# A two-layer graph transformer on one core: v and half of q in another PSUM pool, weights on a second queue, a drained first block and a light second one

## The chip, the core and the metric

The kernel runs on one core of one Trainium2 chip. A core has TensorE (matrix products into PSUM), VectorE, ScalarE and GpSimd for the rest, and SyncE, which here only issues transfers. Each engine carries out its own instructions in order. Transfers are issued from the instruction streams of SyncE, ScalarE and GpSimd; an issue that has to wait holds up what stands behind it in that stream. The metric is device time in microseconds (us), the median of three runs.

## What is computed

Two graph-transformer layers on 2708 tokens of width 512, 8 heads of 64, an adjacency matrix (int32, 2708 x 2708) as mask, and a feed-forward part of width 2048:

```python
mask = adj.astype(jnp.float32) + jnp.eye(n, dtype=jnp.float32)
q = (h @ Wq.T + bq).reshape(n, N_HEADS, D_K)
k = (h @ Wk.T + bk).reshape(n, N_HEADS, D_K)
v = (h @ Wv.T + bv).reshape(n, N_HEADS, D_K)
scores = jnp.einsum('nhd,mhd->hnm', q, k) / jnp.sqrt(jnp.float32(D_K))
scores = jnp.where(mask[None, :, :] == 0, jnp.float32(-1000000000.0), scores)
attn = jax.nn.softmax(scores, axis=-1)
ctx = jnp.einsum('hnm,mhd->nhd', attn, v).reshape(n, D_MODEL)
h1 = _layer_norm(h + ctx @ Wo.T + bo, ln1_g, ln1_b)
ff = jax.nn.relu(h1 @ W1.T + b1) @ W2.T + b2
h2 = _layer_norm(h1 + ff, ln2_g, ln2_b)
```

(The line of `h1` joins two lines of the reference.) An entry of the matrix is set with probability of about 0.3%, so a token has few neighbours.

## The kernel before, in words

The work is done per tile of 128 tokens: 22 tiles, the last with 20. Attention is not a matrix product here. For each token the kernel lists its neighbours, sorts the tokens by the length of their lists, and gathers the k and v rows of the neighbours. A place in the list is a slot; tile g of the sorted order has `CAPS[g]` slots, 22 for tile 0 down to 3 for tile 21. An attention step ("chunk") takes up to two slots: GpSimd gathers kv rows (`gather`, L948), VectorE multiplies with q and sums per head (L987, L993), ScalarE takes exponentials (L1006) and scales v (L1013), VectorE scales one slot and adds (L1019, L1026). Behind a tile's last chunk come `sums` (L1034 to L1049) and `divided` (ScalarE, L1057), which leaves `cx`. `loads` gathers up to three chunks ahead, into five buffers.

The program has these stages.

- **Keys** (`first`, layer 0). For each tile, k and v by `project` (L565), each four matmuls of 128x512 into one PSUM tile with tag "g", of which there are three (`ps`). VectorE adds the bias to k (L834), ScalarE copies v (L836) and issues the store of the row pair. Beside this the adjacency rows come in (L652), GpSimd adds the diagonal (L653), ScalarE squares them into codes (L657), and VectorE finds the largest codes (`lists`, L660 to L667). When all tiles have their lists, `counted` and `ranked` compute each token's rank; 22 indirect transfers (L765) scatter the lists to their places in DRAM, one load reads them back (L776), and `ident_i` (L791) then says which token stands where.
- **Queries** (`first_queries`, layer 0). q for all tiles in their original order, biased by VectorE (L880) and stored in pairs (`written`, L868). At tile 9 (`OWN`) the rows of the first block's tokens (`xr`, gathered by `ident_i`) are transposed and their queries computed, at tile 11 those of the second block, which go to the table `q_own`. `beside_queries` loads w1 and w2, advances the attention and, at tiles 17 and 18, starts the first block's attended part.
- **Blocks**, for each layer: the sorted tiles in pairs, 11 blocks. Block 0 is (21, 20), 148 tokens; the others have 256. The attended part of a block (`attended`): `cx` transposed, multiplied by Wo (o), residual and norm. The feed-forward part (`feed_forward`): 16 steps f, each four matmuls into a PSUM tile pf of tag "f" (three of them, pool `ps_f`), ReLU by ScalarE into ft (L1266), and with a lag of three steps two matmuls of W2 into the sums a0 and a1 (L1246). Within the steps of block k the attention of the block after it is moved on: `advance` gives it credit, at most two finished tiles may stand ready, and at f = 10 `through(k + 1)` takes what is missing. In layer 0, `keys_values` makes k and v of the layer after it from the finished block.
- **Between the layers**: the queries of the first 8 sorted tiles from preloaded `zT` tiles, then 8 more by `queries`, each with a load of `zT` from DRAM, a projection, VectorE's bias (L1191) and a store.

TensorE, ScalarE and SyncE run in the order in which the program is written. VectorE and GpSimd are ordered by a scheduler, except where the program names them too (GpSimd in the first two stages, VectorE in the queries stage and between the layers). The order of the blocks and the drain of the attention stand in these lines:

```python
blocks = [(NT - 1, NT - 2)] + [
    (i, NT - 3 - i) for i in (*range(5, 8), *range(5), *range(8, NT // 2 - 1))
]
```

So block 1 is (5, 14), with 11 + 8 = 19 slots, and (0, 19), with 28, is block 4. A projection's four matmuls show as eight records in the trace.

## Time and profile before

| | us |
|---|---|
| median of 3 runs | 2006.14 (2004.35 to 2006.95) |
| the profiled execution | 2007.56 |
| its span, first to last instruction | 2005.7 |
| TensorE busy | 1910.0 |
| VectorE busy | 1302.4 |
| ScalarE busy | 935.2 |
| GpSimd busy | 800.3 |

The mean granted clock of TensorE is 0.983 of its full rate. The transfers moved 367.98 MB, 183 GB/s on average, but 322 and 348 GB/s in the first two stretches of 50 us, where the adjacency rows come in. Of the chain of work that ended last the trace gives only the end, some 4 us: the second tile's norm, its `rd` on GpSimd, and the store of the output. Busy times of several engines lie beside each other and don't add up to the span; where TensorE is idle, the trace names what released it (`<-`), and that is how its rows are read: start, length, engine, line, operation, how many records, and in brackets the idle time before them with its releaser.

### The profile page before, as it was taken

The page shows a single profiled execution, that of the slowest core. Times are in us where ns is not written, and L with a number is a line of the kernel's source. Part 1 is how long each engine was busy: PE and PEld are TensorE (multiplying, and loading weights), DVE is VectorE, ACT ScalarE, POOL GpSimd, SP SyncE. Part 2 cuts the span into 40 slices and gives each one's busy share as a digit, 9 for nine tenths or more (in the row PEclk, how much of TensorE's full clock was granted, in tenths as well). Part 3 has the DMA queues.
Part 4 walks back from the last instruction along what each step waited for, and adds up shares of the span by engine and source line. Part 5 has one row for each costly group of instructions (what it writes and reads, how often), then busy time and mean ns, then how long its engine had stood idle before and what let it go on. Part 6 is the DMA issues. An engine that isn't in the chain of part 4 may idle for free. (4 is left out here: it accounts for less than half of the span.)

```text
span 2005.7 us, 20899 instructions
## 1 busy us (share of the span) xinstructions
PE 1910.0 (95%) x6162; PEld 1102.3 (55%) x6162; DVE 1302.4 (65%) x2140; ACT 935.2 (47%) x3219; POOL 800.3 (40%) x708
## 2 busy tenths in 40 slices
PE   8989887999999999999999996999999999999996
PEld 3434334556655566556566642456666666666664
DVE  6874387866878668477542027697699879776421
ACT  4560145563664537446432112566467555664310
POOL 3104345544645436345210023454385546544110
PEclk9999998999999999999999998999999999999998
DMA  8985768545566456455310647666467556454000
GB/s 321 349 296 193 253 227 320 184 160 194 173 210 200 164 177 198 138 181 167 128 56 19 220 153 256 216 211 219 152 220 242 195 172 231 163 184 147 27 11 13
DMA packets 131615, 367.98 MB, mean 183 GB/s; under 512 B 16796, under 2 KB 36620, under 8 KB 128782
## 3 DMA queue, kind: packets, MB, share of 16 engines
q0 software_dynamic: 69104, 246.35, 36.7%
q1 hardware_dynamic: 59332, 109.10, 15.8%
q10 hardware_dynamic: 3054, 11.09, 1.4%
q8 instruction: 50, 0.82, 0.2%
q14 instruction: 75, 0.61, 0.1%
HBM read 315.14 MB, written 51.35 MB: 183 GB/s over the span
## 5 line engine op out<-in xcount | busy, mean ns | idle before, releaser
L948 POOL DMA_INDIRECT kv<-kv_d,idx x420 | 552.0, 1314 | 501.9 <-DVE acc L1026 343.8
L1246 PE MATMUL a<-w,ft 128*128 128x512 f32 (+1 forms) x1408 | 666.3, 598 | 2.0 <-ACT ft L1266 1.3
L1258 PE MATMUL pf<-hT,w 128*128 128x256 f32 (+1 forms) x2816 | 636.9, 373 | 22.0 <-ACT ft L1266 14.8
L1258 PEld LDWEIGHTS pf<-hT,w 128*128 128x128 f32 x2816 | 520.7, 191 | 202.4 <-issue 106.3
L1246 PEld LDWEIGHTS a<-w,ft 128*128 128x128 f32 (+1 forms) x1408 | 255.6, 186 | 227.2 <-issue 203.1
L1266 ACT ACTIVATE ft<-pf,b 128x256 f32<-128x256 f32 (+1 forms) x352 | 157.6, 459 | 426.5 <-PE pf L1258 419.5
L987 DVE TENSOR_TENSOR kv<-kv,q 128x1024 f32<-128x1024 f32 (+3 forms) x222 | 256.6, 1159 | 147.2 <-DMA kv<-kv_d,idx 130.9
L1013 ACT ACTIVATE kv<-kv,p 128x64 f32<-128x64 f32 x1232 | 311.1, 335 | 5.0
L993 DVE TENSOR_REDUCE sc<-kv 128x16 f32<-128x1024 f32 (+3 forms) x222 | 254.8, 1153 | 1.2
L1026 DVE TENSOR_TENSOR acc<-acc,kv 128x1024 f32<-128x1024 f32 (+2 forms) x178 | 204.0, 1146 | 38.7 <-ACT kv L1013 37.5
L1006 ACT ACTIVATE p<-sc,minus 128x8 f32<-128x8 f32 (+1 forms) x420 | 103.5, 295 | 204.4 <-DVE sc L993 178.7
L1086 POOL TENSOR_TENSOR rd<-va,mhalf 128x1 f32<-128x1 f32 (+1 forms) x88 | 81.5, 927 | 283.5 <-DVE va L1084 281.3
L1019 DVE TENSOR_TENSOR kv<-kv,p 128x512 f32<-128x512 f32 (+1 forms) x178 | 121.7, 684 | 74.2 <-ACT p L1006 74.2
L565 PE MATMUL o<-wo,cT 128*128 128x512 f32 (+1 forms) x352 | 155.1, 593 | 0.5 <-ACT cT L1101 0.5
L565 PEld LDWEIGHTS o<-wo,cT 128*128 128x128 f32 (+1 forms) x352 | 65.1, 186 | 86.5 <-issue 74.2
L1057 ACT ACTIVATE cx<-acc,su 128x64 f32<-128x64 f32 (+1 forms) x352 | 88.6, 334 | 33.7 <-DVE su L1049 30.1
L1277 DVE TENSOR_TENSOR h<-a,h 128x512 f32<-128x512 f32 (+1 forms) x44 | 28.9, 680 | 111.7 <-PE a L1246 111.7
L1090 DVE SCALAR_TENSOR_TENSOR h<-h,rd,ln_b 128x512 f32<-128x512 f32 (+1 forms) x88 | 65.8, 748 | 53.2 <-POOL rd L1086 53.2
L660 DVE MAX8 tops<-code 128x8 f32<-128x247 f32 (+2 forms) x242 | 82.9, 402 | 19.0 <-ACT code L657 18.8
L657 ACT ACTIVATE code<-aj 128x2708 bf16<-128x2708 int32 (+1 forms) x22 | 73.2, 3328 | 45.5 <-POOL aj L653 41.3
L1316 POOL DMA_INDIRECT kv_d<-kvs,ident_i x22 | 22.9, 1042 | 179.1 <-ACT kvs L1310 117.8
L1013 ACT ACTIVATE acc<-kv,p 128x64 f32<-128x64 f32 (+1 forms) x352 | 88.8, 335 | 1.4
(132 smaller groups left out, 1531.0 us busy)
## 6 DMA issues: line engine op xcount, KB each, us to landing
aj<-in_adj SPq DMA_DIRECT2D x21, 1354.0 KB
w<-in_W SPq DMA_DIRECT2D x32, 512.0 KB
kv_d<-kvs ACTq DMA_DIRECT2D x21, 512.0 KB
xg<-in_xT SPq DMA_DIRECT2D x20, 512.0 KB
kv<-kv_d,idx POOLq DMA_INDIRECT x420
q_d<-qs SPq DMA_DIRECT2D x22, 256.0 KB
zT_d<-zT SPq DMA_DIRECT2D x22, 256.0 KB
xb_d<-h SPq DMA_DIRECT2D x21, 256.0 KB
```

Source lines behind the costliest of these rows:

```text
L565: nc.tensor.matmul(o[:r], xs(c), wm[:, c, :], start=(c == 0), stop=(c == NC - 1))
L948: nc.gpsimd.indirect_dma_start(out=to, out_offset=None, in_=table[:, :], in_offset=bass.IndirectOffsetOnAxis(ap=s, axis=0), bounds_check=N ...
L987: nc.vector.tensor_tensor(kv[:r, :c, :DM], kv[:r, :c, :DM], self.q[:r].unsqueeze(1).to_broadcast([r, c, DM]), ALU.mult,)
L993: nc.vector.tensor_reduce(self.sc[:r, s0 : s0 + c, :], kv[:r, :c, :DM].rearrange("p s (h d) -> p s h d", d=DK), AX.X, ALU.add,)
L1006: nc.scalar.activation(p[:r, s, :], self.sc[:r, s, :], AF.Exp, bias=minus[:r, g, s : s + 1])
L1013: nc.scalar.activation(to[:, i, hd], kv[:r, i, DM + h * DK : DM + (h + 1) * DK], AF.Copy, scale=p[:r, s0 + i, h : h + 1],)
L1019: nc.vector.tensor_tensor(to[:, 0, :].rearrange("p (h d) -> p h d", d=DK), kv[:r, 0, DM:].rearrange("p (h d) -> p h d", d=DK), p[:r, s0, : ...
L1026: nc.vector.tensor_tensor(self.acc[:r, :c, :], self.acc[:r, :c, :], kv[:r, :c, DM:], ALU.add)
L1057: nc.scalar.activation(cx[:r, hd], self.acc[:r, 0, hd], AF.Copy, scale=self.su[:r, h : h + 1])
L1246: nc.tensor.matmul(a[:r], fts[f][:, c0 : c0 + r], self.w2[f // 2][:, f % 2, :], start=(f == 0), stop=(f == NFC - 1),)
L1258: nc.tensor.matmul(pf[:, :w], self.w1[f // 2][:, c, f % 2 * P : f % 2 * P + P], hT[:, c, :w], start=(c == 0), stop=(c == NC - 1),)
L1266: nc.scalar.activation(ft[:, :w], pf[:, :w], AF.Relu, bias=self.b1[:, f : f + 1])
```

## The change

- **PSUM.** v of every tile in the keys stage, and q of every second tile in the queries stage, go to pool `ps_f` (tag "f") instead of `ps`; pf takes 512 columns there, as they do.
- **Order in the first stages.** The transposition of `bk` comes behind the first k; `ranked` comes behind the last tile's k instead of the tile before it; `written` stores a pair of q at the next even tile instead of two pairs later, ahead of that tile's load of tokens.
- **Queues.** w1 and w2 are loaded from the last two tiles of the keys on (parts 0 and 1, SyncE) and in the first three of the queries (parts 2 to 4, ScalarE), instead of at every second query; Wk and Wv of the layer after it go on ScalarE, each in one transfer.
- **Blocks.** Block 1 is (19, 18), with 13 slots. Behind block 0's last tile three empty steps let its attention finish before the next tile begins. The first block's attended part starts at tiles 15 and 16 of the queries instead of 17 and 18.
- **Between the layers**, `zT` is loaded three ahead instead of two.
- **End of a block.** The last three steps of W2 are done per tile: all of a0, then all of a1.

```diff
...
     def chunked(ap):
         return ap.rearrange("(c p) n -> p c n", p=P)
 
-    def matrix(w, name, tag):
+    def matrix(w, name, tag, by=None):
         src = chunked(w[name])
         t = wts.tile([P, src.shape[1], src.shape[2]], F32, tag=tag, name=tag)
+        if by:
+            by.dma_start(out=t, in_=src)
+            return t
         k = max(1, src.shape[1] // 4)
         for c in range(0, src.shape[1], k):
             nc.sync.dma_start(out=t[:, c : c + k, :], in_=src[:, c : c + k, :])
...
             nc.tensor.matmul(pr[:, c * P : (c + 1) * P], ones, dg[:, c, :], start=True, stop=True)
         nc.vector.tensor_copy(t, pr)
 
-    def project(xs, r, wm, name):
-
-        o = ps.tile([P, DM], F32, tag="g", name=name)
+    def project(xs, r, wm, name, other=False):
+
+        o = (ps_f if other else ps).tile([P, DM], F32, tag="f" if other else "g", name=name)
         for c in range(NC):
             nc.tensor.matmul(o[:r], xs(c), wm[:, c, :], start=(c == 0), stop=(c == NC - 1))
         return o
...
         wk = matrix(w, "Wk", "wk")
         turning = turned_row(cols[1], "bk", 1.0)
         bk = next(turning)
-        finish(turning)
         wv = matrix(w, "Wv", "wv")
         pa = tc.tile_pool(name="pa", bufs=2)
         lists, counted, ranked, listed = lists_of(pa.__enter__())
...
             xs = tokens(t, 0)
             kv = wts.tile([P, 2 * DM], F32, tag=f"w2_{5 + t % 3}", name="kvs")
             k = project(xs, r, wk, "k")
+            if t == 0:
+                finish(turning)
             nc.vector.tensor_tensor(kv[:r, :DM], k[:r], bk[:r], ALU.add)
-            v = project(xs, r, wv, "v")
+            if t == NT - 1:
+                ranked(*counts)
+            v = project(xs, r, wv, "v", other=True)
             nc.scalar.copy(kv[:r, DM:], v[:r])
             if before:
                 nc.scalar.dma_start(**before)
...
                 if done == NT:
                     counts = counted()
             meanwhile(t)
-            if t == NT - 2:
-                ranked(*counts)
             if t == QT:
                 wq = matrix(w, "Wq", "wq")
                 turning = turned_row(cols[0], "bq", DK**-0.5)
...
 
         for t in range(NT):
             r = size(t)
-            q = project(tokens(t, 1), r, wq, "q")
+            if t % 2 == 0 and made:
+                written()
+            q = project(tokens(t, 1), r, wq, "q", other=t % 2 > 0)
             if t % 2 == 0:
                 qs = wts.tile([P, 2, DM], F32, tag=f"w2_{5 + t // 2 % 3}", name="qs")
                 made.append((t, qs))
             nc.vector.scalar_tensor_tensor(
                 qs[:r, t % 2], q[:r], DK**-0.5, bq[:r], ALU.mult, ALU.add
             )
-            if len(made) > 2:
-                written()
             if t == OWN - 1:
                 listed()
                 pa.__exit__(None, None, None)
...
-        def load_w1(self, j):
+        def load_w1(self, j, by=nc.sync):
             t = wts.tile([P, NC, 2 * P], F32, tag=f"w1_{j}", name="w1")
-            nc.sync.dma_start(
+            by.dma_start(
                 out=t, in_=chunked(self.w["W1"])[:, :, 2 * P * j : 2 * P * (j + 1)]
             )
             self.w1.append(t)
 
-        def load_w2(self, j):
+        def load_w2(self, j, by=nc.sync):
             t = wts.tile([P, 2, DM], F32, tag=f"w2_{j}", name="w2")
-            nc.sync.dma_start(out=t, in_=chunked(self.w["W2"])[:, 2 * j : 2 * j + 2, :])
+            by.dma_start(out=t, in_=chunked(self.w["W2"])[:, 2 * j : 2 * j + 2, :])
             self.w2.append(t)
 
         def load_second(self, part, temp):
...
 
             zTs = []
             for i in range(len(tiles) + 1):
-                while len(zTs) < min(i + 2, len(tiles)):
+                while len(zTs) < min(i + 3, len(tiles)):
                     zT = dn.tile([P, NC, P], F32, tag="cT", name="zT", bufs=3)
                     nc.sync.dma_start(out=zT, in_=zT_d[self.n][tiles[len(zTs)]])
                     zTs.append(zT)
...
             accs = [ps_a.tile([P, DM], F32, tag=f"a{i}", name=f"a{i}") for i in range(len(block))]
             fts = []
 
-            def second(f):
+            def second(f, only=None):
                 c0 = 0
                 for g, a in zip(block, accs):
                     r = size(g)
+                    if only not in (None, g):
+                        c0 += r
+                        continue
                     nc.tensor.matmul(
                         a[:r],
                         fts[f][:, c0 : c0 + r],
...
                     c0 += r
 
             for f in range(NFC):
-                pf = ps_f.tile([P, 2 * P], F32, tag="f", name="pf")
+                pf = ps_f.tile([P, DM], F32, tag="f", name="pf")
                 for c in range(NC):
                     nc.tensor.matmul(
                         pf[:, :w],
...
                 if f >= LAG:
                     second(f - LAG)
                 yield None
-            for f in range(NFC - LAG, NFC):
-                second(f)
+            for g in block:
+                for f in range(NFC - LAG, NFC):
+                    second(f, g)
             zs = []
             for g, a, h in zip(block, accs, hs):
                 r = size(g)
...
     now = Layer(0, layers[0])
 
 
-    blocks = [(NT - 1, NT - 2)] + [
-        (i, NT - 3 - i) for i in (*range(5, 8), *range(5), *range(8, NT // 2 - 1))
+    blocks = [(NT - 1, NT - 2), (NT - 3, NT - 4)] + [
+        (i, NT - 5 - i) for i in (*range(8, 5, -1), *range(6))
     ]
     NB = len(blocks)
     order = [g for block in blocks for g in block]
...
         peak = small.tile([P, NT], F32, tag="peak", name="peak", bufs=1)
         nc.vector.memset(peak, 0.0)
         loaded = loads(n)
-        steps = [(g, s0, c, i) for g in order for i, (_, s0, c) in enumerate(chunks_of(g))]
+        steps = []
+        for g in order:
+            cuts = chunks_of(g)
+            steps += [(g, s0, c, i, i + 1 == len(cuts)) for i, (_, s0, c) in enumerate(cuts)]
+            if g == order[1]:
+                steps += [None] * 3
+        steps += [None] * 3
         kv = next(loaded)
         yield 0.0
         q = asked(n, order[0])
-        done = []
-        for k in range(len(steps) + 3):
-            if k < len(steps):
-                g, s0, c, i = steps[k]
+        done = [None] * 3
+        for k, step in enumerate(steps):
+            if step:
+                g, s0, c, i, last = step
                 if i == 0:
                     t = Tile(g, q)
                 if k > 0:
...
                 t.weights(kv, s0, c)
                 if i == 1 and g != order[-1]:
                     q = asked(n, order[order.index(g) + 1])
-                done.append((t, kv, s0, c, i + 1 == len(chunks_of(g))))
-            if 0 < k <= len(steps):
-                t1, kv, s0, c, _ = done[k - 1]
-                t1.weigh(kv, s0, c)
-            if 1 < k <= len(steps) + 1 and done[k - 2][-1]:
-                done[k - 2][0].sums(peak)
-            if k > 2 and done[k - 3][-1]:
-                t3 = done[k - 3][0]
-                got[t3.g] = t3.divided()
-            yield steps[k][2] / SLOTS if k < len(steps) else 0.5
+                done.append((t, kv, s0, c, last))
+            else:
+                done.append(None)
+            t3, t2, t1 = done[-4:-1]
+            if t1:
+                t1[0].weigh(*t1[1:4])
+            if t2 and t2[-1]:
+                t2[0].sums(peak)
+            if t3 and t3[-1]:
+                got[t3[0].g] = t3[0].divided()
+            yield c / SLOTS if step else 0.2
...
             now.load_first()
         if t > NT - 3:
             now.load_second(t + 2 - NT, temp)
+            now.load_w1(t + 2 - NT)
+            now.load_w2(t + 2 - NT)
 
     def beside_queries(t):
 
-        if t % 2 == 0 and len(now.w2) < 5:
-            now.load_w1(len(now.w1))
-            now.load_w2(len(now.w2))
+        if len(now.w2) < 5:
+            now.load_w1(len(now.w1), nc.scalar)
+            now.load_w2(len(now.w2), nc.scalar)
         if t > OWN:
-            advance(1.0 if t < NT - 5 else 0.6)
-        if t == NT - 5:
+            advance(1.0 if t < NT - 7 else 0.45)
+        if t == NT - 7:
             through(0)
             early[0] = now.attended(blocks[0], got)
             next(early[0])
-        if t == NT - 4:
+        if t == NT - 6:
             for _ in blocks[0]:
                 next(early[0])
 
...
                 if not last:
                     if (k, f) == (0, 10):
                         now.load_next()
-                        now.kv = [matrix(nxt.w, "Wk", "wk")]
-                    if (k, f) == (0, 14):
-                        now.kv.append(matrix(nxt.w, "Wv", "wv"))
+                        now.kv = [matrix(nxt.w, "Wk", "wk", nc.scalar)]
+                    if (k, f) == (0, 13):
+                        now.kv.append(matrix(nxt.w, "Wv", "wv", nc.scalar))
                     if (k, f) == (3, 2):
                         now.wq = matrix(nxt.w, "Wq", "wq")
                     if f == 1 and k in (1, 3):
```

## The prediction

> **What bounds the kernel now.** I read the page first, then the windows by stage, then TensorE's waits and the timelines of its longest ones.
>
> ```profile
> PE 1910.0 (95%) x6162; PEld 1102.3 (55%) x6162; DVE 1302.4 (65%) x2140; ACT 935.2 (47%) x3219; POOL 800.3 (40%) x708
> ...
> PEclk9999998999999999999999998999999999999998
> ```
>
> TensorE is busy for 1910.0 of 2005.7 us, and the change removes no matmul. So at most the 95.7 us of TensorE idle time can go, and what low clock adds behind it. The windows say where it lies (edges: first query matmul, first matmul of layer 0's feed-forward part, its second block, layer 1's first queries, its feed-forward part, that part's middle, the last matmul). After the window's edges and length come TensorE's busy us, its matmuls, then the other engines; PEclk is the first figure after POOL.
>
> ```profile
> 0.00:178.59 178.59, 162.57 (x376) 70.18 (x376) 134.71 (x470) 84.36 (x44) 29.34 (x68) 0.99 0.83 297
> 178.59:304.35 125.76, 107.72 (x257) 44.30 (x256) 64.66 (x92) 30.05 (x118) 58.85 (x57) 0.95 0.71 237
> 304.35:376.40 72.05, 62.48 (x224) 30.81 (x225) 57.62 (x80) 38.63 (x152) 43.63 (x35) 0.91 0.81 287
> 376.40:1188.83 812.43, 804.61 (x2681) 486.20 (x2680) 481.44 (x694) 375.82 (x1375) 311.13 (x250) 1.00 0.47 158
> 1188.83:1269.97 81.14, 62.79 (x145) 26.13 (x143) 50.32 (x71) 20.47 (x83) 27.09 (x24) 0.89 0.59 204
> 1269.97:1310.00 40.03, 37.55 (x154) 20.44 (x154) 32.87 (x41) 31.37 (x127) 21.41 (x18) 1.00 0.90 296
> 1310.00:1989.90 679.90, 672.30 (x2329) 424.19 (x2328) 475.97 (x684) 354.50 (x1323) 305.01 (x254) 1.00 0.47 158
> ```
>
> Length minus busy: 16.0, 18.0, 9.6, 7.8, 18.4, 2.5, 7.6 us, and 15.8 behind the last matmul. Three quarters of the span hold only 15.4 us; the change must earn its gain in the seams. TensorE's timeline there (idle before, and releaser, in brackets; one projection is 8 records, 3.43 us apart when nothing waits):
>
> ```profile
> 205.95 10.57 PE L565 MATMUL q<-wq,xg 128*128 128x512 f32 x24 [3.05 <-DVE qs L880]
> 221.94 0.58 PE L1096 MATMUL tp<-ident,xr 20*128 20x20 f32 x4 [5.43 <-DMA xr<-in_x,ident_i]
> 296.58 5.24 PE L565 MATMUL q<-wq,xg 128*20 128x512 f32 x8 [4.36 <-DVE h L1219]
> 331.49 2.34 PE L1258 MATMUL pf<-hT,w 128*128 128x148 f32 x8 [6.57 <-ACT ft L1266]
> 1228.52 5.26 PE L565 MATMUL q<-wq,zT 128*128 128x512 f32 x8 [11.70 <-DMA zT<-zT_d]
> ```
>
> The second line hides a chain that is independent of TensorE's pace; GpSimd's timeline shows it:
>
> ```profile
> 173.98 1.11 POOL L765 DMA_INDIRECT rec_d<-rec,ranks  x1 [18.40 <-DVE ranks L761]
> 205.02 1.50 POOL L776 DMA_DIRECT2D new<-rec_d  x1 [3.12 <-DMA rec_d<-rec,ranks]
> 215.01 0.48 POOL L791 CAST ident_i<-new 128x22 int32<-128x22 f32 x1 [7.92 <-DMA new<-rec_d]
> ```
>
> Ranks, 22 scatters 1.28 us apart, a read-back, the cast, the gather of `xr`: 48 us from 173.98 to the flip at 221.94.
>
> **The change, step by step**
>
> **A. Up to the first flip.** Keys: v moves to the other three PSUM buffers, so k and v no longer wait for each other's evacuation. Nine such waits (2.94 at 63.1, then 0.2 to 1.4 each) go: 9.2 us, plus 1.8 for the half-speed matmuls at 63.11 (5.40 us for 8 records against 3.60). Moving `bk`'s transposition behind the first k gives under 1 us, since the 4.7 us before it cover the weights' arrival. But this does not reach the end. The ranks need VectorE's `before` (done at 165.5), and the lists before it are paced by the adjacency rows (DMA 83% busy in that window), which the change doesn't touch. What shifts: the rank matmuls ran at 169.75 behind a v; now they stand behind the short k of the last tile, which is done by then, and start when k's evacuations free PSUM, at about 166.5. VectorE then has two bias sums and one evacuation (0.7 us each, now ahead of the ranks) before the ranks: about 170.5 instead of 173.5, **-3 us**. A read-back now meets less traffic: the loads of w1/w2 stood at 206 and 211 to 214, and now all go out by about 180. The 7.92 us wait is bounded by itself above and by the 3.12 us of the scatters' landing below; I take 5, so **-3 us**. Flip at about 216. TensorE has its ten queries done near 205 (start 171, 10 x 3.43; the 3.05 us wait goes because `written` stores a pair two tiles earlier, so buffers return; SyncE now waits at that store for VectorE's qs with the next xg load behind it, which is for queries four tiles, 13.7 us, later), and waits some 11 us instead of 5.4. So 14 us of gains upstream become 6. A: **-6** (-3 to -10).
>
> Two rules of the Trainium skill weigh here. The page "DMA: Bandwidth & Descriptors", section "Issuing engines are not separate DMA queues", says that DMAs from ScalarE and SyncE share the same DMA engines, so a second issuer saves issue time only. By it, w1/w2 on ScalarE's queue are worth their issue (0.5 us each on SyncE, hidden): nothing. The rows agree on bandwidth, but the timing moves: 3 MB leave the window of the read-back, and that is the 3 us above; by the rule alone A is -3. The other, "TensorE: Matmul & The Clock Gate", section "What's actually happening", has the clock halve after an idle window of about 3.4 us. By it, the short waits cost no clock. The rows differ: after 2.94 us at 63.1, and after only 1.75 us at 271.75, 8 records took 5.40 and 5.16 us. I follow the rows: each removed wait of 2 us or more brings 1.6 to 1.8 us more.
>
> **B. First flip to the first feed-forward matmul (82.4 us).** The first block's drain takes two steps of the third tile (kv x q and its sum, 2 x 2.44 us at 257 and 261) from in front of its last sums, so `cx` is ready near 262 on the old clock (268.5 before) and the attended part can start two tiles earlier, behind q of tile 15 (262.4). Then q16, two o, and q17 to q21 (17.2 us) cover the norm chain (15 us from the last o to h: 285.2 to 300.3), which two queries could not. Gone: 0.34 + 1.75 + 1.6 (clock) + 4.36 + 1.6 (clock) + 1.07 + 0.4 = **-11** (-5 to -13). New coupling: q of odd tiles holds `ps_f` buffers that the first three pf need; VectorE's order puts q21's evacuation some 3 us behind its matmul: below 1 us.
>
> **C. Layer 0's first block.** 9.6 us of waits for ft plus about 4.6 of low clock (320.0 to 337.5). ScalarE stood behind p, p behind VectorE, VectorE 7.21 us behind the gather of q, which waits for every q_d store. The next block is now (19, 18): 13 slots instead of 19, its queries from `q_own`. But the gather for tile 8 follows in the same stretch, at about the same distance from the last store (VectorE evacuates q21 some 3 us into the block). I keep 6 of 14: **-8** (-2 to -13).
>
> **D. Layer boundary.** TensorE needs 36.2 us from 1216.7 to 1252.9 for four projections (13.7): 17.3 of waits, 4.6 of clock. Looking three ahead, zT of the third query loads with the first two (1193.6), and the 11.70 goes. The load after it now needs TensorE to free the first's buffer, and SyncE holds the q_d stores behind it meanwhile; both come from work that precedes it. What is late next: the evacuations. `query` still has only three PSUM buffers, and in the changed order VectorE does three chunks of tile 19 before it frees the preloaded queries' buffers (19.5 us of its work from 1208 put these at about 1217 and 1228 to 1230). I get waits of 4, 8.7 and 1.5 us, the last projection ending near 1244.3, less 1.6 for clock: **-7** (0 to -17).
>
> **E.** Layer 1's first block: one 2.48 us wait for ft, fewer slots: -1 (+2 to -2.5).
>
> **F.** Tail: summing per tile lets the first tile finish 1.7 us earlier (4 records of 0.43), so its store leaves GpSimd free before the second's `rd` (it stood from 1993.9 to 1995.3): -1.5 (-0.5 to -2.5). **Elsewhere** the blocks' order changes; the heavy tile 0 now has 29 slots in its block instead of 28; wk and wv go on ScalarE, 0.5 us of issue each with one ft behind; summing per tile wants the last ft 1.7 us sooner, still 3.4 us behind its pf: 0 (-6 to +6).
>
> **Sum:** -6 - 11 - 8 - 7 - 1 - 1.5 = -34.5. The profiled execution took 2007.56 us (span 2005.7 and 1.9 around it): 1973. It lay 1.4 above the median shown, 2006.14, so I predict **1971 us**.
>
> **Rivals**
> 1. *The waits go whole* (24%). For: each has a named cause that an edit meets. Against: VectorE's order at the boundary. A -8, B -11, C -13, D -14, E -2, F -2: -50, 1956 us.
> 2. *They are only replaced* (12%). q's gather still holds C, PSUM holds D, the read-back is no faster: A -3, B -11, C -2, D 0, F -1.5: -17.5, 1988 us.
> 3. *VectorE becomes the bound in the middle* (4%): slower. A chunk costs it 4.4 us (1.16 + 1.15 + 0.68 + 1.15 by its rows, and idle); 29 slots are 15 chunks, 65 us, and norms and evacuations some 16: 81 of a block's 82. Place: blocks 2 to 10 in both layers, where the backlog starts one light block later. With 3.5 us per block in place of the 15.4 us there now: 18 x 3.5 - 15.4 - 34.5 = +13, 2019 us. It decides above 2.8 us per block (49.9 / 18). Against: only the heavy block showed such waits (2.2 and 2.3 us).
> 4. *The drain doesn't drain* (2%): in the changed VectorE order tile 19's chunks still stand before the last sums at the boundary. Then D is 0 or worse and B half: -20, 1986 us.
>
> **How the numbers follow.** Likeliest 58%, rivals as above. Its own range is 1962 to 1982. With rivals 1, 2 and 4, and the bounds of A, C and D (all good -58, all poor -8), the 8-in-10 range is 1950 to 1990. What a measurement can tell from no change is 0.2%, 4 us. Faster 0.94, same 0.02, slower 0.04.
>
> **What would show it.** A: first flip near 216 with a wait of about 11 us, rank scatters from 171; a flip at 222 refutes it, one below 210 means the lists were not DMA-paced. B: 71 us from flip to feed-forward, no wait at q21. C: a wait for ft below 6 us. D: no wait on zT's DMA above 2 us, instead VectorE's qs as releaser. F: 14 us behind the last matmul. It is wrong if windows of the middle blocks show more than 15 us of new idle time.

## The result, and the profile after

| | before | after |
|---|---|---|
| time, median of 4 runs each | 2006.55 us (2004.35 to 2008.01) | 1983.8 us (1979.94 to 1985.18) |
| after / before | | 0.9884, 95% interval 0.9867 to 0.9902 |
| span of the profiled execution | 2005.7 us | 1982.0 us |

The time lies inside the range and in the forecast direction; 34.5 us were forecast for the profiled span and 23.7 came. The first line of the page of after:

```profile
PE 1903.5 (96%) x6162; PEld 1104.5 (56%) x6162; DVE 1303.1 (66%) x2140; ACT 934.6 (47%) x3219; POOL 798.3 (40%) x708
```

The matmuls are the same; TensorE's busy time fell by 6.5 us (fewer of them ran at low clock; the mean granted clock is 0.985, where it was 0.983) and its idle time from 95.7 to 78.5. To compare many kernels I cut the span at events that each of them has: the first flip of `xr`, the first `pf` of layer 0, the first flip of `h` behind its first block, layer 1's first query, its first `pf`, the flip of `h` behind its first block, the last matmul. (The prediction's windows ended the first blocks and the middle elsewhere, so lengths differ a little from those there.) The windows of after with these edges, columns as in the prediction:

```profile
0.00:213.55 213.55, 195.53 (x457) 85.71 (x457) 141.81 (x483) 84.76 (x45) 53.09 (x93) 0.98 0.87 305
213.55:290.37 76.82, 68.69 (x176) 28.38 (x177) 46.48 (x68) 24.14 (x96) 31.51 (x28) 0.94 0.61 203
290.37:351.95 61.58, 54.75 (x204) 30.46 (x205) 51.66 (x73) 34.06 (x134) 36.08 (x30) 0.93 0.82 290
351.95:1152.58 800.63, 790.01 (x2645) 479.32 (x2643) 493.10 (x700) 382.53 (x1405) 312.93 (x258) 1.00 0.50 163
1152.58:1248.11 95.53, 83.64 (x201) 35.05 (x200) 45.61 (x72) 18.43 (x72) 28.04 (x24) 0.95 0.52 182
1248.11:1305.23 57.12, 57.12 (x221) 30.15 (x221) 51.61 (x69) 41.16 (x164) 32.48 (x26) 1.00 0.84 286
1305.23:1968.75 663.52, 653.70 (x2263) 415.40 (x2261) 469.01 (x669) 349.56 (x1305) 300.81 (x250) 1.00 0.48 158
```

The same cuts for both kernels, in us, beside the terms of the prediction's sum:

| stage | before | after | difference | predicted |
|---|---|---|---|---|
| A, start to first flip | 221.94 | 213.55 | -8.4 | -6 |
| B, to the first `pf` | 82.41 | 76.82 | -5.6 | -11 |
| C, layer 0's first block | 65.12 | 61.58 | -3.5 | -8 |
| middle of layer 0 | 797.39 | 800.63 | **+3.2** | 0 |
| D, layer boundary | 103.11 | 95.53 | -7.6 | -7 |
| E, layer 1's first block | 60.27 | 57.12 | -3.2 | -1 |
| rest of layer 1 | 659.54 | 663.52 | **+4.0** | 0 |
| F, behind the last matmul | 15.92 | 13.25 | -2.7 | -1.5 |

So B and C brought less, and two stretches that should not have moved cost 7.2 us. TensorE's timeline at the seams, with the wait in front of each group and its releaser:

```profile
213.55 0.58 PE L1100 MATMUL tp<-ident,xr 20*128 20x20 f32 x4 [6.79 <-DMA xr<-in_x,ident_i]
216.68 1.09 PE L1100 MATMUL tp<-ident,xr 128*128 128x128 f32 x4 [2.55 <-DMA xr<-in_x,ident_i]
...
290.37 6.88 PE L1265 MATMUL pf<-hT,w 128*128 128x148 f32 x32 [5.21 <-ACT hT L1105]
313.20 2.34 PE L1265 MATMUL pf<-hT,w 128*128 128x148 f32 x8 [4.84 <-ACT ft L1273]
319.88 1.27 PE L1265 MATMUL pf<-hT,w 128*128 128x148 f32 x8 [1.99 <-ACT ft L1273]
...
1202.20 5.40 PE L568 MATMUL q<-wq,zT 128*128 128x512 f32 x8 [3.45 <-DVE qs L1195]
1213.49 5.57 PE L568 MATMUL q<-wq,zT 128*128 128x512 f32 x8 [5.89 <-DVE qs L1195]
1220.59 10.54 PE L568 MATMUL q<-wq,zT 128*128 128x512 f32 x24 [1.53 <-DMA zT<-zT_d]
```

The line at 290.37 is new: 5.21 us for `hT`, and the 32 matmuls behind it took 6.88 us. In the kernel before they took 4.32:

```profile
304.35 4.32 PE L1258 MATMUL pf<-hT,w 128*128 128x148 f32 x32 [0.46 <-ACT hT L1101]
```

ScalarE's timeline of after says why:

```profile
286.87 0.49 ACT L1010 ACTIVATE p<-sc,minus 128x8 f32<-128x8 f32 x2 [10.26 <-DVE sc L997]
287.39 2.02 ACT L1017 ACTIVATE kv<-kv,p 128x64 f32<-128x64 f32 x8
289.32 1.77 ACT L1105 ACTIVATE hT<-tp,b 128x20 f32<-128x20 f32 x8
```

The flips of `h` started at 283.95, and ScalarE was idle, but next in its queue stood `p` of a chunk of the second block, whose scores VectorE made only behind the two norms. VectorE's timeline has the end of the second norm and the scores:

```profile
282.50 0.75 DVE L1094 SCALAR_TENSOR_TENSOR h<-h,rd,ln_b 128x512 f32<-128x512 f32 x1 [0.47 <-POOL rd L1090]
...
285.61 1.22 DVE L997 TENSOR_REDUCE sc<-kv 128x16 f32<-128x1024 f32 x1
```

On GpSimd the chain of ranks began at the time forecast; its wait for the read-back shrank by less than the 3 us assumed (5.76 against 7.92):

```profile
170.92 1.11 POOL L768 DMA_INDIRECT rec_d<-rec,ranks  x1 [17.54 <-DVE ranks L764]
200.49 1.51 POOL L779 DMA_DIRECT2D new<-rec_d  x1 [1.65 <-DMA rec_d<-rec,ranks]
208.32 0.48 POOL L794 CAST ident_i<-new 128x22 int32<-128x22 f32 x1 [5.76 <-DMA new<-rec_d]
```

### The profile page after: what moved, and what is told of

It reads as the page before. It is cut to its first block, busy times and chain, and to the rows that moved or that the text cites. A ratio compares the mean times of both kernels' runs of the same rounds, so it can differ in the third digit from the quotient of the medians.

```text
span 1982.0 us, 20873 instructions
## 1 busy us (share of the span) xinstructions
PE 1903.5 (96%) x6162; PEld 1104.5 (56%) x6162; DVE 1303.1 (66%) x2140; ACT 934.6 (47%) x3219; POOL 798.3 (40%) x708
## 3 DMA queue, kind: packets, MB, share of 16 engines
q1 hardware_dynamic: 55780, 103.86, 15.3%
## 5 line engine op out<-in xcount | busy, mean ns | idle before, releaser
L1090 POOL TENSOR_TENSOR rd<-va,mhalf 128x1 f32<-128x1 f32 (+1 forms) x88 | 85.7, 974 | 270.0 <-DVE va L1088 268.6
L1094 DVE SCALAR_TENSOR_TENSOR h<-h,rd,ln_b 128x512 f32<-128x512 f32 (+1 forms) x88 | 65.8, 748 | 48.1 <-POOL rd L1090 48.1
L568 PE MATMUL k<-wk,xg 128*128 128x512 f32 (+1 forms) x176 | 82.1, 611 | 6.8 <-DMA wk<-in_Wk 6.7
```

The lines of the kernel that those rows point to most:

```text
L568: nc.tensor.matmul(o[:r], xs(c), wm[:, c, :], start=(c == 0), stop=(c == NC - 1))
```

## The experiments

Each kernel is the changed one with the edit shown. The runs came in four groups; within a group kernels share a chip and the runs of the kernel before (medians 2000.5, 2004.1, 2002.0 and 2003.0 us), so across groups ratios are compared. Stage lengths are of one profiled execution, in us.

| run | time | ratio (95% interval) | A | B | C | middle | D | E | rest |
|---|---|---|---|---|---|---|---|---|---|
| e_w | 1979.9 | 0.9902 (0.9884 to 0.9920) | 210.6 | 76.2 | 61.9 | 799.9 | 96.9 | 57.1 | 663.4 |
| e_psum | 1986.8 | 0.9943 (0.9924 to 0.9961) | 216.3 | 80.4 | 57.8 | 801.7 | 93.9 | 57.1 | 662.5 |
| e_qown | 1979.7 | 0.9908 (0.9890 to 0.9926) | 209.6 | 76.9 | 61.3 | 800.1 | 93.8 | 57.1 | 664.9 |
| e_query_psum | 1983.2 | 0.9914 (0.9893 to 0.9934) | 211.5 | 76.6 | 63.1 | 799.5 | 97.3 | 57.1 | 665.2 |
| after_again | 1981.2 | 0.9880 (0.9865 to 0.9895) | 213.5 | 77.4 | 62.3 | 800.1 | 95.0 | 57.1 | 663.5 |
| e_hold | 1983.6 | 0.9894 (0.9877 to 0.9911) | 213.0 | 78.6 | 58.5 | 801.3 | 94.8 | 57.1 | 665.2 |
| e_region | 1980.9 | 0.9882 (0.9867 to 0.9897) | 209.7 | 77.4 | 60.8 | 800.8 | 87.4 | 58.6 | 670.5 |
| e_tail_last | 1981.2 | 0.9882 (0.9867 to 0.9897) | 213.7 | 76.7 | 63.1 | 799.3 | 94.5 | 57.1 | 663.4 |
| e_blocks | 2008.6 | 1.0031 (1.0012 to 1.0050) | 208.8 | 79.4 | 65.8 | 798.6 | 98.0 | 70.3 | 675.6 |
| hold_region | 1982.9 | 0.9895 (0.9866 to 0.9923) | 210.9 | 72.7 | 58.4 | 808.3 | 95.3 | 57.1 | 665.2 |
| best_q | 1980.9 | 0.9889 (0.9861 to 0.9918) | 209.8 | 73.0 | 58.4 | 806.1 | 90.5 | 58.6 | 670.7 |
| late_zT | 1991.7 | 0.9943 (0.9925 to 0.9961) | 212.6 | 76.5 | 62.6 | 799.9 | 100.9 | 57.1 | 665.0 |

Start with after_again, the changed kernel once more: each of its stages lies within 0.8 us of the first profile. A differs by up to 5 us between the eleven profiles whose code up to the first flip is the same (208.8 to 213.7; all but e_w and e_psum), so in A only larger differences count.

> The changed kernel itself, as the yardstick of this chip: ratio to the kernel before 0.987 to 0.990, the wait of 5.2 us for hT and those of 3.5 and 5.9 us for VectorE's qs at the layer boundary as in its first profile.

**e_w: the queue of w1 and w2.**

```
-            now.load_w1(t + 2 - NT)
-            now.load_w2(t + 2 - NT)
...
-        if len(now.w2) < 5:
-            now.load_w1(len(now.w1), nc.scalar)
-            now.load_w2(len(now.w2), nc.scalar)
+        if t % 2 == 0 and len(now.w2) < 5:
+            now.load_w1(len(now.w1))
+            now.load_w2(len(now.w2))
```

> w1/w2 of layer 0 go back to SyncE's queue, one pair every second query, everything else as in the changed kernel. Theory (term of step A: the read-back meets less traffic when 3 MB leave its window): the wait of the cast for the read-back returns from 5.8 us towards the 7.9 of the kernel before, the first flip comes 2 to 3 us later (near 216) and the time is 2 to 3 us above the changed kernel's 1983.8. Rival (only issue time moves): the flip stays within 1 us of 213.6 and the time within 1 us.

The flip came at 210.6, and the wait of the cast in GpSimd's timeline was shorter, not longer:

```profile
197.51 1.51 POOL L779 DMA_DIRECT2D new<-rec_d  x1 [1.60 <-DMA rec_d<-rec,ranks]
203.15 0.48 POOL L794 CAST ident_i<-new 128x22 int32<-128x22 f32 x1 [3.57 <-DMA new<-rec_d]
```

While the read-back ran, SyncE issued two of these loads in e_w, 1 MB, and four in the kernel before, 2 MB (206.26 to 212.13); the 3 MB of the prediction are too many. One pair of traces settles little here: over the eleven profiles with the code of the changed kernel the wait of the cast lies between 3.35 and 6.98 us. But the effect of 2 to 3 us that the theory expected shows neither in the wait nor in the time (0.9902; e_qown and e_query_psum beside it 0.9908 and 0.9914), so of the rival the core stands: where these loads are issued gains nothing that can be seen. What set the 7.92 us of before stays open.

**e_psum: one pool of three buffers for k, v and q.**

```
-            v = project(xs, r, wv, "v", other=True)
+            v = project(xs, r, wv, "v")
...
-            q = project(tokens(t, 1), r, wq, "q", other=t % 2 > 0)
+            q = project(tokens(t, 1), r, wq, "q")
```

> All k, v and q back in the one PSUM pool of three buffers, everything else as in the changed kernel. Theory (the keys' waits do not reach the end, the chain of ranks does): the keys end some 9 to 11 us later, TensorE's wait in front of the first flip shrinks by as much, the flip comes 0 to 4 us later and the time is 0 to 4 us above 1983.8. Rival (the keys stage sets the end): the flip and the time are 9 to 14 us later.

The flip came at 216.3, 2.8 us behind after_again and 4.8 to 6.7 behind the other three of its group, so at the upper end of the theory's 0 to 4 or above it. But waits of only 4.8 us returned among the keys, not 9 to 11, and TensorE's wait at the flip did not shrink. B grew by 2.9, with a wait for `h` in front of the last queries, and C shrank by 4.6, chiefly since the wait for `hT` (0.54 us here) left no low clock behind it:

```profile
278.73 2.08 PE L568 MATMUL q<-wq,xg 128*128 128x512 f32 x2 [4.57 <-DVE h L1223]
```

The median lies 3.6 to 7.1 us above those of the three kernels beside it, which have the new pools. The stages show less: A, B and C together are 1.1 us longer than in after_again. So the move is worth a few us by the time, which the stages of one execution explain only in part, and less than the rival's 9 to 14.

**e_qown: the second block's queries kept in SBUF**, against the wait for `hT`. In after VectorE idled 6.85 us near 261, released by a late load from `q_own`.

```
-                    own_query(g, zT, to.get(g, xr), bq, wq)
+                    if g == blocks[1][0]:
+                        own[g] = to[g] = at.tile([P, DM], F32, tag="q", name="q", bufs=QB)
+                    elif g == blocks[1][1]:
+                        own[g] = to[g] = xr
+                    own_query(g, zT, to[g], bq, wq)
...
-            nc.sync.dma_start(out=q_own[g * P : g * P + r, :], in_=to[:r])
```

> The queries of tiles 19 and 18 stay in SBUF (one in the third q buffer, one in xr's), with no store to q_own and no load from it. Theory (the new wait for hT in front of layer 0's feed-forward part comes from VectorE's 6.85 us wait for a q_own load that SyncE issued late): VectorE does not idle near 261 to 268, the 5.21 us wait for hT falls below 1 us, the low clock behind it goes, and the time is 5 to 8 us below 1983.8. Rival 1 (hT is late because ScalarE and VectorE have more work there than TensorE): the wait stays above 4 us and the time within 1 us of 1983.8. Rival 2 (the gain is given back at the next gather of q in the first block): hT's wait goes and the waits for ft there grow by as much, time 0 to 2 us below.

```profile
262.53 1.23 DVE L992 TENSOR_TENSOR kv<-kv,xr 128x1024 f32<-128x1024 f32 x1 [9.45 <-DMA kv<-kv_d,idx]
```

VectorE waited all the same, 9.45 us, now for the gather of `kv` in the same place, and the wait for `hT` was 4.36. The theory falls: the load that the profile named was one of two things late there, and removing it uncovered the other. ScalarE's order was unchanged, which leads to e_hold.

**e_query_psum: six buffers for the boundary's queries.**

```
-                    self.query(tiles[i], zTs[i])
+                    self.query(tiles[i], zTs[i], other and i % 2 > 0)
...
-            q = project(lambda c: zT[:, c, :r], r, self.wq, "q")
+            q = project(lambda c: zT[:, c, :r], r, self.wq, "q", other)
...
-                    now.query(*pool.pop(0))
+                    now.query(*pool.pop(0), len(pool) % 2 > 0)
```

> At the layer boundary every second query goes to the other PSUM pool, so six buffers in place of three; the order of instructions is that of the changed kernel on every engine. Theory (step D: evacuations by VectorE hold the three buffers): the waits of 3.45 and 5.89 us for VectorE's qs go, unless zT's buffers are next, and the boundary takes 65 to 69 us in place of 73.6, the time 4 to 9 us below 1983.8. Rival (zT is freed by the same queries, and SyncE's queue is next): a wait for zT's DMA of 4 us or more takes their place, time within 2 us of 1983.8.

The rival, in full: both waits for `qs` went, and one for `zT` took their place, of 14.79 us. TensorE's line, and SyncE's that explains it:

```profile
1218.46 12.49 PE L568 MATMUL q<-wq,zT 128*128 128x512 f32 x24 [14.79 <-DMA zT<-zT_d]
```

```profile
1192.84 19.23 SPq L1205 DMA_DIRECT2D q_d<-qs  x3
1212.16 0.38 SPq L1182 DMA_DIRECT2D zT<-zT_d  x1
```

SyncE issues three `q_d` stores over 19 us, each when VectorE has made its `qs`, and the loads of `zT` stand behind them. PSUM and the queue are two waits for one thing, VectorE.

**e_region: VectorE's own order kept longer.** The order written by hand ended with the boundary, and the scheduler moved chunks of tile 19, emitted later, in front of its `qs`.

```
-            with tc.manual_schedule(engines={mybir.EngineType.DVE}):
+            hand = tc.manual_schedule(engines={mybir.EngineType.DVE})
+            hand.__enter__()
...
+            if n > 0 and k == 0:
+                hand.__exit__(None, None, None)
             if not last:
                 behind = now.keys_values(block, zs)
```

> VectorE's hand-written order of the layer boundary is kept through layer 1's first block, so tile 19's chunks can no longer be moved in front of the boundary's qs; the queries keep their three buffers. Theory (the boundary's waits of 3.45 and 5.89 us are for qs that stand behind tile 19's chunks on VectorE; three buffers are enough once they don't): at most one wait above 1 us is left among the queries, the boundary takes 62 to 67 us in place of 73.6, and layer 1's first block pays back 0 to 4 us; time 4 to 11 us below the changed kernel's. Rival (three buffers or the loads of zT hold the queries anyway): waits of 5 us or more stay, time within 2 us.

D fell by 7.6 us against after_again. Two waits above 1 us are left among the queries, with no low clock behind them, and three buffers were enough:

```profile
1201.51 3.70 PE L568 MATMUL q<-wq,zT 128*128 128x512 f32 x8 [2.64 <-DVE qs L1195]
1208.15 3.67 PE L568 MATMUL q<-wq,zT 128*128 128x512 f32 x8 [2.94 <-DVE qs L1195]
```

But E rose by 1.5 and the rest by 7.0. The time is the same. The mechanism of D is shown; that this further gain reaches the end is refuted.

**e_tail_last: the sums per tile in the last block alone.**

```
-            for g in block:
+            if self.n == NL - 1 and block == blocks[-1]:
+                for g in block:
...
+            else:
+                for f in range(NFC - LAG, NFC):
+                    second(f)
```

> The sums of the last three f go per tile only in the last block of the last layer; in the other 21 blocks they alternate between the tiles as before the change. Theory (summing per tile wants the last ft 1.7 us sooner, and this is what the 9.5 us of new waits of a for ft are): waits of a for ft fall from 9.5 us to below 3, the stretch behind the last matmul stays near 13.1 us, time 5 to 9 us below the changed kernel's. Rival (these waits come from the blocks' order, with more slots beside each block): they stay above 6 us, or come back as waits of pf for ft, time within 2 us.

TensorE's waits in sum (total, times, longest), after_again first, then e_tail_last:

```profile
PE a L1253 <- ACT ft L1273: 9.4, 9, 2.8
...
PE pf L1265 <- ACT hT L1105: 7.2, 4, 5.2
```

```profile
PE pf L1265 <- ACT hT L1105: 14.2, 11, 5.2
...
PE a L1253 <- ACT ft L1273: 2.0, 2, 1.1
```

`a` waits 7.4 us less for `ft`, and the next block's `pf` 7.0 more for `hT`: ScalarE is late at a block's end by the same amount, and the order of TensorE only decides which matmul meets it. The middles did not move (-0.9 and -0.1).

**e_hold, then hold_region: hT ahead of the second block's third chunk.**

```
-            advance(1.0 if t < NT - 7 else 0.45)
+            advance(1.0 if t < NT - 7 else 0.0)
```

> In the last seven queries of layer 0 the attention of the second block isn't advanced (credit 0 in place of 0.45), so ScalarE's order has hT and the first two ft ahead of tile 19's third chunk. Theory (hT is late because ScalarE stands in order behind a p whose scores VectorE makes only after the two norms): the 5.2 us wait for hT and the low clock behind it go, step B ends 6 to 8 us earlier; the held chunks move into the first block, where the waits for ft may grow by 0 to 4 us; time 2 to 8 us below the changed kernel's. Rival (VectorE has more work there than TensorE, so what is held comes back whole): the waits for ft in the first block grow by 6 us or more, time within 1 us of the changed kernel's or above it.

The wait for `hT` fell to 0.54 us, and C lost the low clock (58.5). But the scheduler moved the held chunks in front of the first block's last sums, and a new wait for `cx` made B 1.2 us longer:

```profile
258.25 1.91 PE L1100 MATMUL tp<-ident,cx 128*128 128x128 f32 x4 [3.25 <-ACT cx L1061]
```

hold_region adds e_region's edit for layer 0 (there for GpSimd's order too):

> As in the run before with credit 0 beside the last queries of layer 0, and VectorE's hand-written order (and GpSimd's) is kept through layer 0's first block, so the held chunks can't be moved in front of the first block's last sums. Theory (hT's wait goes when ScalarE has it ahead of tile 19's third chunk, and the 3.25 us wait for cx of that run was the moved chunks): neither wait is above 1 us, step B takes 68 to 71 us in place of 77; of that the first block pays back 0 to 6 us and the middle 0 to 3; time 2 to 8 us below the changed kernel's. Rival (whatever is held comes back whole): first block and middle together 6 us or more longer, time within 1 us of the changed kernel's.

B fell to 72.7, near the prediction's 71, and C to 58.4; together 8.6 us are gone against after_again. The middle took 8.2 of them back: `a` waited 2.76 us for `ft` in the second block, which it had not done in after, and `v` later 2.74 for VectorE (1.73 in after), each with low clock behind it. TensorE's timeline of hold_region:

```profile
283.66 4.31 PE L1265 MATMUL pf<-hT,w 128*128 128x148 f32 x32 [0.55 <-ACT hT L1105]
...
348.06 5.50 PE L1253 MATMUL a<-w,ft 128*20 128x512 f32 x8 [2.76 <-ACT ft L1273]
...
711.84 6.76 PE L568 MATMUL v<-wv,zT 128*128 128x512 f32 x8 [2.74 <-DVE kvs L1316]
```

The cause of the wait is shown; the rival is right about the sum.

**e_blocks: the old order of the blocks.**

```
-    blocks = [(NT - 1, NT - 2), (NT - 3, NT - 4)] + [
-        (i, NT - 5 - i) for i in (*range(8, 5, -1), *range(6))
+    blocks = [(NT - 1, NT - 2)] + [
+        (i, NT - 3 - i) for i in (*range(5, 8), *range(5), *range(8, NT // 2 - 1))
     ]
```

> The order of the blocks is that of the kernel before (the second block is the one of tiles 5 and 14, 19 slots, not 19 and 18, 13 slots); drain, PSUM, queues and the sums per tile stay as changed. Theory (the light second block is worth step C and layer 1's first block; the middle's loss of 4 us per layer belongs to the new order, which puts the heavy tiles in the later blocks): layer 0's first block takes 3 to 8 us longer than the changed kernel's 62, layer 1's first block 2 to 4 longer than 57, the two middles together 5 to 9 us shorter than 800 and 663; the sum within 3 us of the changed kernel's time. Rival (the middle's loss comes from elsewhere): middles unchanged within 2 us, time 5 to 12 us above.

The time rose above that of the kernel before. Layer 0's first block took 3.5 us longer than in after_again, as the theory had it. In the middle of layer 0, 1.5 of 2.7 us came back, so the order of the blocks is a part of that loss, in the place the theory named and smaller. The cost sits in layer 1, which it did not expect: the first block took 70.3 us, 10 more than in the kernel before, mostly in one wait:

```profile
1296.14 1.91 PE L1100 MATMUL tp<-ident,cx 128*128 128x128 f32 x4 [10.65 <-ACT cx L1061]
```

Drained, the attention starts its second block three steps later: between the boundary's first query and the first `pf`, VectorE did ten chunks here and twelve in the kernel before. With 13 slots that block is still ready in time; with 19 it isn't. The rest of layer 1 lost 12 us more, in waits of 0.2 to 3 us and low clock. So the changed kernel needs the light second block, which neither theory had. That the drain is what needs it is argued from the order of the steps: no run leaves out the drain alone, and the boundary, 5 us shorter than in the kernel before, leaves the attention less time too.

**best_q** joins hold_region, e_region and e_qown.

> Three things at once: layer 0's held second block with VectorE's order kept through the first block, the same order kept through layer 1's first block, and the queries of tiles 19 and 18 left in SBUF. Theory (each removes its own wait, B -7, D -8, and what they pay back in the blocks behind is under half): ratio to the kernel before 0.982 to 0.986, 4 to 12 us below the changed kernel's. Rival (the middle takes back whatever the seams gain): ratio 0.987 to 0.989.

B, C and D are 13 us shorter together than in after_again; middle, E and rest 15 us longer. The rival holds. None of these versions is faster than the changed kernel by more than the interval.

**late_zT: two parts undone, in different stages.**

```
-        if t == NT - 7:
+        if t == NT - 5:
...
-        if t == NT - 6:
+        if t == NT - 4:
...
-                while len(zTs) < min(i + 3, len(tiles)):
+                while len(zTs) < min(i + 2, len(tiles)):
```

> Two parts undone, in different stages: layer 0's first block takes its attended part two queries later (at tile 17's query, as before the change), and at the layer boundary zT is loaded two ahead in place of three. Theory (each part is worth what its stage shows): a wait of 3 to 5 us for h in front of the last queries returns and step B is 2 to 6 us longer than the 77 of the changed kernel; a wait of 8 to 12 us for zT's DMA returns and the boundary is 5 to 9 us longer than its 95; the stretches behind both unchanged within 2 us; time 7 to 15 us above the changed kernel's. Rival (what a seam loses the blocks behind it win back, as the held attention of the runs before showed in reverse): the two middles are together 4 to 9 us shorter, time 1 to 6 us above.

```profile
1200.99 3.70 PE L568 MATMUL q<-wq,zT 128*128 128x512 f32 x8 [3.22 <-DVE qs L1195]
1220.04 15.47 PE L568 MATMUL q<-wq,zT 128*128 128x512 f32 x32 [15.34 <-DMA zT<-zT_d]
```

TensorE's timeline at the boundary: the wait for `zT` returned, longer than forecast (15.34 us), D grew by 5.9, nothing behind it won that back, and the span of the profiled execution is 5.8 us longer than after_again's. By the ratios the loss is some 13 us; no stage shows the rest. B did not change (-0.9): the wait for `hT` went, since the held third chunk fell behind `hT` in ScalarE's order, and small waits came (1.65 for `xg`, 0.89 for `h`). The expectation for B was wrong: with the drain in place, three queries cover the norm chain (11.6 us from the last `o` to `h`, where the prediction took 15 from the old profile).

## Why the prediction was right or wrong

The errors lay on both sides: B, C and the two long stretches came out 17.1 us worse than forecast, the other terms 6.4 us better, and so the sum missed by only some 11.

**A (-6; -8.4).** The keys' gains stay upstream, as argued: waits of 6.79 and 2.55 us stand at the flip, and in e_psum the freed PSUM is worth 3 to 7 us there, not 9 to 14. That the scatters started at 170.92, where 171 was forecast, is luck in part. The step's first -3 took the lists as done at 165.5 and put the ranks 5 us behind them. VectorE's timeline, before and then after, from the lists' last step to the ranks:

```profile
164.84 0.71 DVE L722 TENSOR_TENSOR before<-before,run 128x528 f32<-128x528 f32 x1
171.17 0.69 DVE L1140 TENSOR_TENSOR ln_b<-ln_b,temp 128x512 f32<-128x512 f32 x1 [1.73 <-DMA temp<-in_bo]
173.50 0.18 DVE L761 CAST ranks<-at 128x22 int32<-128x22 f32 x1
```

```profile
162.65 0.71 DVE L725 TENSOR_TENSOR before<-before,run 128x528 f32<-128x528 f32 x1
168.11 0.69 DVE L1144 TENSOR_TENSOR ln_b<-ln_b,temp 128x512 f32<-128x512 f32 x1 [2.37 <-DMA temp<-in_bo]
170.44 0.18 DVE L764 CAST ranks<-at 128x22 int32<-128x22 f32 x1
```

The lists came 2.2 us sooner, and the way from them to the ranks shrank by 0.9, from 8.0 to 7.1 us: a bias sum ahead of the ranks waits for the load of its row, which the prediction counted at nothing. Four of the eleven profiles with this code have the flip at 208.8 to 209.8, below the 210 that was to mean that the lists are not paced by DMA. That sign misleads: there too GpSimd waits for the last adjacency rows, which only came sooner (it adds their diagonal at 140.2 to 141.4; at 143.9 in after and 145.4 in the kernel before). The other term, "a read-back now meets less traffic: -3", had the wrong cause; e_w shows no such effect. On it the rule of the Trainium skill ("DMA: Bandwidth & Descriptors", "Issuing engines are not separate DMA queues": a second issuer saves issue time only) was the better guide to the cause than my reading of the row, though the -3 for all of A that it alone would have given is further from the measured -8.4.

**B (-11; -5.6).** The named waits all went. The failed step is the new coupling, put "below 1 us" and sought in PSUM. It was on ScalarE: the chunks advanced beside the last queries put a `p` ahead of `hT`, for 5.2 us here and 2.6 us of low clock counted in C. e_hold, which holds these chunks, removes both, and hold_region, which also keeps the order of VectorE and GpSimd, reaches 72.7.

The largest of the waits that went, 4.36 us for `h`, went for another reason than the earlier start. It ended with the line that reads o out of PSUM (VectorE's timeline of before):

```profile
295.85 0.67 DVE L1219 TENSOR_TENSOR h<-o,xb 128x512 f32<-128x512 f32 x1
```

In e_psum, with the early start and the old pool, it is back (4.57 us, the same line); in late_zT, with the late start and the new pool, it is not, and B is not longer. So it was a wait for o's PSUM buffer, and the first block's earlier start, taken with what it does to ScalarE's order, gains nothing in B.

**C (-8; -3.5).** 2.6 us of the shortfall is that clock. The waits for `ft`, 4.84 and 1.99 us, are each below the 6 that was to show; together with some 1.5 us of low clock behind them they come to 8.3, where 6 were kept.

**D (-7; -7.6).** Right in place, size and what was late next: the `zT` wait gone, waits of 3.5, 5.9 and 1.5 us against 4, 8.7 and 1.5, with VectorE's `qs` as releaser. late_zT confirms the cause and that this gain reaches the end.

**E (-1; -3.2) and F (-1.5; -2.7)** were small and on the right side, a little beyond their ranges. E hides a step that the prediction lacked: that layer 1's first block needs a light block behind it (e_blocks, 70.3 us against 57.1).

**Elsewhere (0; +7.2).** The failed term beside B. It lies beyond the range of -6 to +6. I costed the attention that leaves the seams at nothing. It moves into the middle, as the windows show (VectorE's busy time there, and TensorE's idle time, length less busy):

| | VectorE busy | TensorE idle |
|---|---|---|
| middle of layer 0: before | 478.4 | 7.8 |
| e_blocks | 485.7 | 8.8 |
| after | 493.1 | 10.6 |
| e_hold | 497.8 | 11.1 |
| hold_region | 502.8 | 14.7 |
| rest of layer 1: before | 456.3 | 7.6 |
| after | 469.0 | 9.8 |
| e_region | 475.8 | 14.5 |
| e_blocks | 460.0 | 15.3 |

VectorE is busy 62% there, so it isn't a bound; but each chunk that arrives later makes some `ft`, `cx` or `v` late. hold_region and e_region, which hold chunks back and keep the order by hand, raise both in their own layer and leave the other nearly as it was. VectorE's busy time is not the whole of it: in the rest of layer 1, e_blocks has less of it than after and more idle time, by its order of blocks. The prediction's third rival named this place, with 3.5 us of waits per block; 20.4 us over its 18 blocks are 1.1, where there had been 0.9. Not explained is why late_zT, at 496.1, pays no more than the changed kernel in length (799.9).

## What to carry over

Before counting the end of a wait as a gain, look for what its engine was doing meanwhile: work that is only held back returns as waits of 1 to 3 us in a stretch that looked untouched. Where a profile names a releaser, ask what stands second: in three runs here (e_qown, e_query_psum, e_tail_last) the named wait was removed, and others came in its place, in sum nearly as long or longer. And test the parts of a change together with what they lean on: with the old order of blocks, the rest of this change is worth less than nothing.

## What the runs showed of the hardware

Low clock behind a wait didn't follow from the wait's length. The same eight query matmuls at the boundary take 3.60 to 3.70 us at full clock. There, 2.77 us of waiting was followed by 5.22 us (e_blocks), 3.19 by 5.17 (hold_region) and 3.45 by 5.40 (after), but 2.87 by 3.70 (after_again) and 3.22 by 3.70 (late_zT). Earlier, 1.65 us in front of q in late_zT was followed by 5.37. The rule weighed in the prediction ("TensorE: Matmul & The Clock Gate", "What's actually happening", an idle window of about 3.4 us) would put none of these but the 3.45 at low clock; the runs put some of the shorter ones there, so a removed wait of 1.7 to 3.5 us may bring some 1.6 us more or nothing.
